# Routing's product and transposition as two pieces of VectorE's account; merges and output gating may wait a step

## The chip, the cores and the metric

The kernel runs on one core of one Trainium2 chip. The metric is the device time of one execution in microseconds (us), given as the median of several runs.

## The reference

Two batches of 1024 tokens of width 512 go through a layer norm, a causal attention with 32 heads of 16, and a feed-forward part whose output gates that of the attention. All is in float32.

```python
def attn(x):                                   # b, l, d = 2, 1024, 512; h, hd = 32, 16
    q, k, v = (heads(x @ W.T + b) for W, b in ((Wq, bq), (Wk, bk), (Wv, bv)))
    scores = einsum('bhqd,bhkd->bhqk', q, k) / sqrt(hd)
    att = softmax(where(causal, scores, -inf))
    return merge_heads(att @ v) @ Wo.T + bo

def ffn(x):                                    # E = 8 experts of rank R = 16, the best 2 used
    result = x @ W_base.T + b_base
    top_p, top_i = top_k(softmax(x @ W_gate.T), 2)
    route_w = sum(one_hot(top_i, 8) * (top_p / sum(top_p)))
    h = einsum('bnd,erd->bner', x, A)
    return result + einsum('bner,eor->bno', h * route_w[..., None], B) * 1.0

xn = layernorm(x)
return x + attn(xn) * silu(ffn(xn))
```

## The kernel before

Tokens are taken in chunks (b, c) of 512: two batches b, two chunks c of each. Attention is done in units (b, oc, c): eight heads (the output columns oc, 128 wide) for the queries of one chunk, over all keys up to them. A unit of c = 0 has 5 steps, one of c = 1 has 13. A step makes the scores of one or two tiles of 128 keys for four heads on TensorE (tiles `s`, line 1392), their exponentials on ScalarE (two instructions, `pt`, line 1401), and, where the tile lies on the diagonal, a multiplication with the causal mask on VectorE (two instructions). The product with the values (`av`, line 1442) follows one step later, so that TensorE has other work while ScalarE makes the exponentials. The last unit is cut otherwise. There are 144 steps in all, numbered from 0 in the variable `plan`.

The other work is spread over the steps as filling. It is written as generators, one for each piece of work: projections to q and k (products q1 to q7), to values, gate and output (p1 to p7), both by Strassen's scheme of seven products, with sums of operands (`asum`, `wqk`) made on VectorE ahead; the router's product (`ph`, copied to `hl` by ScalarE); layer norm. All filling products write to tiles of one PSUM pool (`ps_mm`) of two buffers, and VectorE, or ScalarE, reads them out.

The order of instructions is written out by a planner in Python when the program is built; the engines then run their instructions in that order. For each step n it emits the scores, the `av` matmuls of step n - 1 (with two copies from PSUM if these close a unit), the masks, and then calls `fill(n)`, which

- takes steps of generators that cost TensorE time (`Task` with a cost) until the step has its share, sorted by due time,
- then runs the list `later` of delayed pieces: (step, function),
- then takes steps of generators that cost TensorE nothing (layer norm, sums, routing) as long as VectorE's account allows. Such a generator is asked again at each `yield PAUSE`, and rests until the next step at `yield WAIT`,
- issues weight loads (`issue_parts`), at most six parts ahead.

VectorE's account is the class `Metered`, through which all VectorE instructions go: it adds 0.09 us and 1/930 us per element of a row for each. `late_by(n + 1, begins, more)` says by how much VectorE would be late for the masks of the next step if `more` us of work were added; `enough` is that question with 0.65. A piece in the list `patient` that is due in this very step is put off by one step when `enough()` is true.

The pieces that the change touches:

- `routed_task` picks the best two experts of every token by a chain of small VectorE operations (128x32), multiplies `hl` with the weights (`hw`, 128x512) and transposes the product in blocks (`hsq`). `hsq` is stored to DRAM and read back as `hwT` a step later (`place`), on the queue SP, which issues nearly all DMAs in order.
- `post` finishes a unit: `spread` brings the sums of the softmax to `dens`, `merge` takes reciprocals (`rc`) and joins the two halves of heads (`avs`, `oT`), `collect` brings the reciprocals back, `finish` multiplies. `merge` and `finish` are `patient`.
- `out_task` projects the attention's output in four blocks (i, j), in the order (0,0), (1,1), (0,1), (1,0). `final(i, j)` follows the read-out of the last product of a block: gating (`x<-x,g`), adding the residual (`x<-x,xr`), the store, and the load of the next residual tile `xr` (a pool of two buffers) if there is one left.
- `gate_task` has the same four blocks with a tanh on ScalarE (`sg`) and a multiplication; `apart`, behind the last q product of a unit, divides qT into two halves by two ScalarE activations (line 707).

Of the kernel before, what the change touches and what calls it, by code (L numbers as in the profile page):

```python
# [12 lines left out]
ALU = mybir.AluOpType  # L13
# [67 lines left out]
def direct(ctx, tc, sound, x, wq, wk, wv, wo, wb, wa, wg, wB, bq, bk, bv, bo, bb, out):  # L81
# [9 lines left out]
    nc = tc.nc  # L91
    ve = Metered(nc.vector)
# [117 lines left out]
    PAUSE = object()  # L210
# [552 lines left out]
    def out_task(k):  # L763

        _, b, c = stages[k]
        y, g = block_of(chunk_tile(b, c)), block_of(g_tiles[b, c])
        order = [(0, 0), (1, 1), (0, 1), (1, 0)]
        xts = {}

        def block(t, i, j):  # L770
            rows = slice(c * C + BK * i, c * C + BK * i + BK)
            return t[b, rows, BK * j : BK * j + BK].rearrange("(t p) o -> p t o", p=P)

        def load():
            i, j = order[len(xts)]
            xts[i, j] = sb.tile([P, 2, BK], F32, tag="xr", name=f"xr_{b}_{c}_{i}{j}")
            nc.sync.dma_start(out=xts[i, j], in_=block(x, i, j))

        def final(i, j):
            ve.scalar_tensor_tensor(y(i, j), y(i, j), 0.5, g(i, j), ALU.mult, ALU.mult)  # L780
            ve.tensor_tensor(y(i, j), y(i, j), xts[i, j], ALU.add)
            nc.sync.dma_start(out=block(out, i, j), in_=y(i, j))
            if len(xts) < 4:
                load()

        load()
        load()
        yield from block_task(k, y, final)
# [3 lines left out]
    def routed_task(b, c):  # L792


        hl = hls.pop((b, c))
        lg = hl[:, :, ER : ER + E]

        def each(name):
            return small.tile([P, TT], F32, tag=name, bufs=1, name=name)

        def every(name):
            return small.tile([P, TT, E], F32, tag=name, bufs=1, name=name)

        def over(t):
            return t.unsqueeze(2).to_broadcast([P, TT, E])

        mx = each("mx")
        ve.tensor_reduce(mx, lg, AX.X, ALU.max)
        pr = every("pr")
        ve.tensor_tensor(pr, lg, over(mx), ALU.subtract)  # L810
        yield WAIT
        nc.scalar.activation(pr, pr, AF.Exp)

        def top(p, n):
            m = each(f"m{n}")
            ve.tensor_reduce(m, p, AX.X, ALU.max)
            key = every(f"key{n}")
            ve.tensor_tensor(key, p, over(m), ALU.is_equal)
            ve.tensor_tensor(
                key, key, rev.unsqueeze(1).to_broadcast([P, TT, E]), ALU.mult  # L820
            )
            k = each(f"k{n}")
            ve.tensor_reduce(k, key, AX.X, ALU.max)
            ve.tensor_tensor(key, key, over(k), ALU.is_equal)
            ve.tensor_tensor(key, key, over(m), ALU.mult)
            return m, key

        m1, r1 = top(pr, 1)
        yield WAIT
        ve.tensor_tensor(pr, pr, r1, ALU.subtract)  # L830
        m2, r2 = top(pr, 2)
        ve.tensor_add(m1, m1, m2)
        ve.reciprocal(m1, m1)
        ve.tensor_add(r1, r1, r2)
        ve.tensor_tensor(r1, r1, over(m1), ALU.mult)
        yield WAIT
        hw = sb.tile([P, TT, ER], F32, tag="hw", bufs=1, name="hw")
        ve.tensor_tensor(
            hw.rearrange("p t (e r) -> p t e r", e=E),
            hl[:, :, 0:ER].rearrange("p t (e r) -> p t e r", e=E),  # L840
            r1.unsqueeze(3).to_broadcast([P, TT, E, R]),
            ALU.mult,
        )
        sq = sb.tile([P, NS, TT, SQ], F32, tag="sq", bufs=1, name="hsq")
        ve.transpose(
            out=sq.rearrange("p q t r -> p t q r"),
            in_=hw.rearrange("p t (q d) -> p t q d", q=NS),
        )
        hwT = sb.tile([P, NS, TT, SQ], F32, tag="hwT", bufs=2, name="hwT")
        scr = dram.tile([NS, SQ, NS, TT * SQ], F32, tag="hscr", name="hscr")  # L850
        nc.sync.dma_start(
            out=scr.rearrange("i d q m -> (i d) (q m)"), in_=sq.rearrange("p q t r -> p (q t r)")
        )

        def place():
            for q in range(NS):
                nc.sync.dma_start(
                    out=hwT[q * SQ : (q + 1) * SQ].rearrange("d i t r -> d i (t r)"),
                    in_=scr[:, :, q].rearrange("i d m -> d i m"),
                )  # L860

        later.append((now[0] + 1, place))
        hwTs[b, c] = hwT
        turned_at[b, c, "h"] = now[0]
# [410 lines left out]
    def late_by(n, begins, more):  # L1275


        free = ve.free + more
        if not 0 < n < len(plan):
            return free - begins  # L1280
        if plan[n - 1][3] and plan[n - 1][0] != units[-1]:
            free = max(free, begins + 2.0) + 1.3
        m = mask_time(n)
        if m:
            free = max(max(free, begins + 2.0) + m / 2, begins + 3.0) + m / 2
        return free - (begins + SV + 1.7 + 0.7)
# [11 lines left out]
    def fill(n):  # L1298


        nonlocal spent
        now[0], begun_at = n, spent
        within = 0 <= n < len(plan)
        causal_here = within and mask_time(n)
        for x in tasks:
            x.waiting = False
        for turn in [turn for turn in turns if turn[0] <= n]:
            turns.remove(turn)
            turn[1]()

        begin = len(plan) - 3
        even = (total - spent) / max(1, len(plan) - n)
        if n == len(plan) - 1:
            even = MM
        if n >= starts[units[-1]] - 8 and n < begin:
            even = sum(x.left for x in tasks if x.steps.__name__ not in ("whole_task", "rest_task"))
            even /= begin - n
        elif n < begin:
            even = min(even, (total - last_work - spent) / (begin - n))
        share = spent + even  # L1320
        if n >= 12:

            left = 0.0
            for x in tasks:
                if x.steps.__name__ in ("whole_task", "rest_task"):
                    continue
                left += x.left
                if x.due > n:
                    share = max(share, spent + left / (x.due - n))
        while True:  # L1330
            free = [x for x in tasks if x.cost and x.released(n)]
            if not free or free[0].due > n + 1:
                due = [x.steps.__name__ for x in tasks if x.cost and x.due <= n + 1]
                if due:
                    assert late, (n, due)
                    turn_late()
                    continue
                if not free or spent + (MM / 2 if causal_here or n < 12 else MM / 8) >= share:
                    break
            task = active[0] if active else free[0]  # L1340
            if (
                task.steps.__name__ == "qk_blocks_task" and task.due > n + 1
                and causal_here and spent - begun_at > 1.5 * MM
            ):

                break
            active[:] = [task]
            ve.ready = clock[0] + SV + spent - begun_at + MM
            cost = task.step()
            if cost is None or cost is WAIT:  # L1350
                task.waiting = True
                active.clear()
            else:
                spent += cost
        ve.ready = 0.0
        begins = clock[0] + max(2.3, SV + spent - begun_at)
        enough = lambda: late_by(n + 1, begins, 0.65) > 0
        for x in [x for x in later if x[0] <= n]:
            if x[0] == n and x[1] in patient and enough():
                continue  # L1360
            later.remove(x)
            x[1]()
        for x in [x for x in tasks if not x.cost]:
            if not x.released(n):
                continue
            said = PAUSE
            while said is not None and said is not WAIT:
                if enough() and x.due > n:
                    break
                said = x.step()  # L1370
            x.waiting = said is WAIT
        clock[0] = begins
        issue_parts()
        for _ in range(1 if active or len(plan) - 5 < n < len(plan) else 2):
            if late and (min(x[0] for x in late) <= n or not within):
                turn_late()
# [586 lines left out]
```

## Time and profile before

| | us |
|---|---|
| three runs, median (lowest, highest) | 601.71 (601.15, 601.98) |
| the profiled execution | 601.97 |
| its span, first to last instruction | 600.2 |
| busy: PE, VectorE (DVE), ScalarE (ACT) | 588.7, 391.6, 319.2 |
| mean granted TensorE clock | 0.996 |

The span is what the engines' records cover; 1.8 us of the profiled execution lie outside it. Matmuls (PE) overlap, and their ends are modelled: a busy PE is not proof of a PE at its peak, so steps are measured from start to start. In a row of the timeline stand the start, the duration, the engine, the line, the operation, the tiles (written <- read), the shape and the number of instructions run together; in brackets the idle time of the engine ahead of it and what ended it. All VectorE instructions have line 55, that of the account's helper, so they are told apart by their tiles. The costliest groups of VectorE are:

```profile
L55 DVE TENSOR_TENSOR pt<-pt,causal 128x512 f32<-128x512 f32 (+1 forms) x160 | 90.6, 582 | 64.9 <-ACT pt L1401 64.7
L55 DVE TENSOR_TENSOR g<-p,g 128x512 f32<-128x512 f32 x28 | 18.9, 686 | 16.8 <-PE p L220 16.5
L55 DVE SCALAR_TENSOR_TENSOR kT<-q,kT 128x256 f32<-128x256 f32 x39 | 16.5, 422 | 14.9 <-PE q L220 14.3
```

The first number behind the bar is the total busy time in us, the second the mean of one instruction in ns, the third the idle time ahead of them.

### The profile page before, as it was taken

What the parts mean: (1) busy time and instruction counts of PE and PEld (TensorE: products, weight loads), DVE (VectorE), ACT (ScalarE), POOL (GpSimd) and SP (SyncE); (2) the same over time, 40 slices, a digit from 0 to 9 for tenths busy, and PEclk for the clock granted to TensorE, in tenths of its full rate; (3) what the DMA queues carried; (4) which work ended last, traced back from release to release, by engine and by line L of the source; (5) the groups of instructions that cost most, each with busy time, mean ns of one, the idle gap of its engine ahead of it and who ended that gap; (6) DMA issues with size and microseconds to landing.
All of it is one profiled execution on the core that took longest, in us unless ns stands there. A gap on an engine that the chain in (4) does not pass through costs nothing.

```text
span 600.2 us, 18801 instructions
## 1 busy us (share of the span) xinstructions
PE 588.7 (98%) x8327; PEld 281.9 (47%) x8327; DVE 391.6 (65%) x821; ACT 319.2 (53%) x368; POOL 9.2 (2%) x26
## 2 busy tenths in 40 slices
PE   8999999999999999999999999999999999999994
PEld 7335344544445544444346544453444454455551
DVE  4546788287488857566487866664547865785742
ACT  2445454656666565556655545455565565565631
POOL 2000000000001000000000000000000000000000
PEclk9999999999999999999999999999999999999998
DMA  8523474247101534234133062430121013401101
GB/s 266 140 69 122 136 261 149 55 142 211 39 4 48 189 109 129 89 101 135 36 111 90 22 194 80 159 125 6 37 71 52 11 51 98 161 21 55 58 20 58
DMA packets 57929, 58.66 MB, mean 98 GB/s; under 512 B 8312, under 2 KB 49280, under 8 KB 57456
## 3 DMA queue, kind: packets, MB, share of 16 engines
q1 hardware_dynamic: 57824, 57.38, 31.0%
q8 instruction: 67, 1.10, 0.8%
q14 instruction: 22, 0.18, 0.1%
q10 hardware_dynamic: 16, 0.00, 0.0%
HBM read 43.24 MB, written 14.12 MB: 96 GB/s over the span
## 4 chain that ended last, share of the span: by engine, by line
PE 93%; DMA 3%; DVE 3%; issue 0%; SPq 0%; ACT 0%; DVEq 0%
PE s L1392 25%; PE av L1442 23%; PE p L220 20%; PE q L220 13%; PE ph L220 3%; PE po L220 2%; PE pv L220 2%; DMA kept<-wqk 1%; PE pq L220 1%; PE pk L220 1%; DMA dens<-den 1%; DMA x<-in_x_dram 1%; DVE wqk L55 1%; PE pq_first L330 1%; PE h L220 1%; PE pk_first L330 0%
## 5 line engine op out<-in xcount | busy, mean ns | idle before, releaser
L1401 ACT ACTIVATE pt<-s 128x1024 f32<-128x1024 f32 x288 | 279.2, 1021 | 230.2 <-PE s L1392 228.6
L1392 PE MATMUL s<-qT,kT 32*128 32x512 f32 (+3 forms) x1680 | 166.5, 490 | 0.1
L1442 PE MATMUL av<-pt,v 128*32 128x512 f32 (+3 forms) x1680 | 154.3, 467 | 0.9 <-DVE pt L55 0.6
L55 DVE TENSOR_TENSOR pt<-pt,causal 128x512 f32<-128x512 f32 (+1 forms) x160 | 90.6, 582 | 64.9 <-ACT pt L1401 64.7
L1392 PEld LDWEIGHTS s<-qT,kT 32*128 32x128 f32 x1680 | 72.4, 184 | 68.3 <-issue 47.3
L1442 PEld LDWEIGHTS av<-pt,v 128*32 128x32 f32 x1680 | 39.7, 108 | 93.6 <-issue 61.4
L220 PE MATMUL p<-wt,asum 128*32 128x256 f32 x960 | 58.2, 379 | 0.0
L220 PE MATMUL q<-asum,wqk 128*32 128x256 f32 x832 | 50.8, 379 | 0.0
L220 PEld LDWEIGHTS p<-wt,asum 128*32 128x32 f32 x960 | 31.0, 110 | 26.5 <-issue 9.9
L220 PE MATMUL q<-xnT,wqk 128*32 128x256 f32 x624 | 40.2, 379 | 0.0
L220 PEld LDWEIGHTS q<-asum,wqk 128*32 128x32 f32 x832 | 27.0, 110 | 25.1 <-issue 8.4
L55 DVE TENSOR_TENSOR g<-p,g 128x512 f32<-128x512 f32 x28 | 18.9, 686 | 16.8 <-PE p L220 16.5
L220 PEld LDWEIGHTS q<-xnT,wqk 128*32 128x32 f32 x624 | 20.9, 110 | 18.9 <-issue 5.1
L220 PE MATMUL p<-w,xnT 128*32 128x256 f32 x448 | 27.3, 379 | 0.0
L55 DVE SCALAR_TENSOR_TENSOR kT<-q,kT 128x256 f32<-128x256 f32 x39 | 16.5, 422 | 14.9 <-PE q L220 14.3
L55 DVE TENSOR_TENSOR x<-p,x 128x512 f32<-128x512 f32 x21 | 14.2, 688 | 15.0 <-PE p L220 15.0
L55 DVE TENSOR_TENSOR v<-p,v 128x512 f32<-128x512 f32 x21 | 14.1, 687 | 11.2 <-PE p L220 11.2
L220 PE MATMUL p<-w,asum 128*32 128x256 f32 x320 | 20.0, 379 | 0.0
L220 PEld LDWEIGHTS p<-w,xnT 128*32 128x32 f32 x448 | 14.5, 110 | 11.1 <-issue 3.3
L747 ACT ACTIVATE sg<-g 128x512 f32<-128x512 f32 x16 | 10.0, 630 | 16.9 <-DVE g L55 16.9
L707 ACT ACTIVATE qT<-qT,half 128x512 f32<-128x512 f32 x26 | 18.8, 722 | 0.4
L220 PE MATMUL ph<-wag_sb,xnT 128*32 128x136 f32 x512 | 17.2, 279 | 0.0
(132 smaller groups left out, 479.4 us busy)
## 6 DMA issues: line engine op xcount, KB each, us to landing
wt<-kept SPq DMA_DIRECT2D x40, 256.0 KB
x<-in_x_dram SPq DMA_DIRECT2D x16, 256.0 KB
scr<-sq SPq DMA_DIRECT2D x6, 512.0 KB
xnT<-scr SPq DMA_DIRECT2D x24, 128.0 KB
w<-in_wb_dram SPq DMA_DIRECT2D x12, 256.0 KB
xr<-in_x_dram SPq DMA_DIRECT2D x12, 256.0 KB
out_dram<-x SPq DMA_DIRECT2D x12, 256.0 KB
w<-in_wv_dram SPq DMA_DIRECT2D x9, 256.0 KB
```

The lines of the kernel that those rows point to most:

```text
L55: return getattr(self.engine, name)(*args, **named)
L220: nc.tensor.matmul(o[j : j + 32], lhsT=lhsT[:, j : j + 32] if len(lhsT.shape) == 2 else lhsT[:, j // 32], rhs=rhs, start=start, stop=stop,)
L330: nc.tensor.matmul(ps[:, cols], lhsT=w[:, k, :], rhs=xnT[:, k, cols], start=k == 0, stop=k == KC - 1)
L707: nc.scalar.activation(qT[:, par], qT[:, 0], AF.Copy, scale=half[:, par : par + 1])
L747: nc.scalar.activation(sg, g(i, j), AF.Tanh, scale=0.5)
L1392: nc.tensor.matmul(ss[s // 2][:, s % 2, col : col + w], lhsT=kT[rows, kt % TT * P : kt % TT * P + P], rhs=qTs[b, oc, c][rows, par, q0 : q0 ...
L1401: nc.scalar.activation(pt[:, 2 * pair : 2 * pair + 2], ss[pair], AF.Exp, scale=0.25)
L1442: nc.tensor.matmul(avs_now[par][32 * s : 32 * s + 32, q0 : q0 + w], lhsT=vs[b, kt][:, h * VS - HD * par : h * VS - HD * par + HP], rhs=pt[ ...
```

## The change

Three edits. In `out_task`, the gating of a block, its residual, store and load become a function `finish` that is put on `later` for this step and marked `patient`, so that it may be put off by one step; at the last block all that are still unfinished are run first. In `routed_task` a `yield PAUSE` stands between the product `hw` and the transposition `hsq`, so the account is asked again between them. In `fill`, the question to patient pieces is asked with 1.35 instead of 0.65 us.

```diff
@@ out_task
         def final(i, j):
-            ve.scalar_tensor_tensor(y(i, j), y(i, j), 0.5, g(i, j), ALU.mult, ALU.mult)
-            ve.tensor_tensor(y(i, j), y(i, j), xts[i, j], ALU.add)
-            nc.sync.dma_start(out=block(out, i, j), in_=y(i, j))
-            if len(xts) < 4:
-                load()
-
+            def finish():
+                ve.scalar_tensor_tensor(y(i, j), y(i, j), 0.5, g(i, j), ALU.mult, ALU.mult)
+                ve.tensor_tensor(y(i, j), y(i, j), xts[i, j], ALU.add)
+                nc.sync.dma_start(out=block(out, i, j), in_=y(i, j))
+                if len(xts) < 4:
+                    load()
+
+            if (i, j) == order[-1]:
+                for x in [x for x in later if x[1] in unfinished]:
+                    later.remove(x)
+                    x[1]()
+                finish()
+            else:
+
+                unfinished.append(finish)
+                patient.append(finish)
+                later.append((now[0], finish))
+
+        unfinished = []
         load()
         load()
         yield from block_task(k, y, final)
@@ routed_task
             r1.unsqueeze(3).to_broadcast([P, TT, E, R]),
             ALU.mult,
         )
+        yield PAUSE
         sq = sb.tile([P, NS, TT, SQ], F32, tag="sq", bufs=1, name="hsq")
@@ fill
-        enough = lambda: late_by(n + 1, begins, 0.65) > 0
+        enough = lambda more=0.65: late_by(n + 1, begins, more) > 0
         for x in [x for x in later if x[0] <= n]:
-            if x[0] == n and x[1] in patient and enough():
+            if x[0] == n and x[1] in patient and enough(1.35):
                 continue
             later.remove(x)
             x[1]()
```

## The prediction

> **What bounds the kernel now.** I read the page first, then the timeline of the matmul engine step by step, then the other engines around each step that is too long. A step is one run of score matmuls `s`, the `av` matmuls of the step ahead, and filling work; steps are counted from 0 at 14.94 us, the first `s` row of the chain.
>
> ```profile
> PE 588.7 (98%) x8327; PEld 281.9 (47%) x8327; DVE 391.6 (65%) x821; ACT 319.2 (53%) x368; POOL 9.2 (2%) x26
> PEclk9999999999999999999999999999999999999998
> PE 93%; DMA 3%; DVE 3%; issue 0%; SPq 0%; ACT 0%; DVEq 0%
> ```
>
> PE is busy 98% of the span at full clock and carries 93% of the chain that ended last. The change adds and removes no instruction on any engine, so only PE's waits can change. They are found by the length of steps: `s` takes 1.07, `av` 0.88, a filling unit (16 records of 256 columns) 0.86. Starts of `s` lie 3.79 apart with two units (504.80 to 508.59), 2.94 with one (508.59 to 511.53), 4.66 with three (352.84 to 357.50). Length is linear in the units, so moving units costs nothing by itself; what a step takes beyond is a wait. Those that the change can reach:
>
> ```profile
> 90.42 0.69 DVE L55 TENSOR_TENSOR hw<-hl,key 128x512 f32<-128x512 f32 x1
> 91.14 0.71 DVE L55 STREAM_TRANSPOSE hsq<-hw 128x512 f32<-128x512 f32 x1
> 91.78 0.72 DVE L55 TENSOR_TENSOR pt<-pt,causal 128x256 f32<-128x256 f32 x2
> 92.30 1.30 PE L1442 MATMUL av<-pt,v 128*32 128x512 f32 x8 [0.60 <-DVE pt L55]
> ...
> 310.37 0.69 DVE L55 SCALAR_TENSOR_TENSOR x<-x,g 128x512 f32<-128x512 f32 x1
> 311.09 0.69 DVE L55 TENSOR_TENSOR x<-x,xr 128x512 f32<-128x512 f32 x1
> 311.70 0.68 DVE L55 COPY oT<-av 128x512 f32<-128x512 f32 x1
> ...
> 312.90 0.75 DVE L55 TENSOR_TENSOR pt<-pt,causal 128x256 f32<-128x256 f32 x2
> 313.46 1.29 PE L1442 MATMUL av<-pt,v 128*32 128x512 f32 x8
> ```
>
> Step 15: `s` starts at 90.56, so `av` could start at 91.63, but VectorE did hw and hsq before the masks. The masks end at 92.50, and the step lasts 4.70: 0.90 lost. Step 73 is the same with the output gating (x<-x,g and x<-x,xr) in front: masks end at 313.65, `av` was due at 313.24, 0.45 lost. In both, the loss is the end of the second mask minus the time `av` was due, plus 0.04. That is my rule below.
>
> ```profile
> 508.59 1.15 PE L1392 MATMUL s<-qT,kT 32*128 32x384 f32 x16
> 509.83 1.94 ACT L1401 ACTIVATE pt<-s 128x1024 f32<-128x1024 f32 x2
> 511.53 1.42 PE L1392 MATMUL s<-qT,kT 32*128 32x512 f32 x8
> ...
> 360.32 2.07 PE L220 MATMUL q<-xnT,wqk 128*32 128x256 f32 x32
> 360.57 0.69 DVE L55 TENSOR_TENSOR v<-p,v 128x512 f32<-128x512 f32 x1 [1.73 <-PE p L220]
> ```
>
> A step with one unit is shorter than ScalarE's loop: the exponentials end at 511.77, the next `s` started at 511.53 and needs both, 0.28 lost. The last two rows show the other wait: filling products share two PSUM buffers, so a product waits until the one before the last is read out (read-out ends at 361.26, the buffer was wanted at 361.18, the step is 0.14 long).
>
> **The change, part by part.** I compared the order of instructions in the two programs as built. PE's order is the same through step 73.
>
> *Hw and hsq as two pieces.* In step 14 the masks now stand between them. They start 0.64 after hw's 90.42 at 91.06 (the gap between hsq and masks now), end at 91.78, against 91.63 plus the rule: 0.18 lost instead of 0.91. Gain 0.73. Hsq moves behind a read-out and four weight sums, to 93.6, and pushes the next masks to end at 95.55, due at 95.61: hidden. Its DMA to DRAM and the four that bring hwT back go one step later on SP, behind a store of sums; hwT is read from step 21 on (114 us), 15 us later. If the four sums took 0.1 more, the next `av` would lose that.
>
> *Output gating may wait.* In steps 71 to 73 it does, twice. The gating of the second block moves from step 71 to 72, that of the third from 72 to 73, where the fourth follows at once. The masks of step 72 come 0.8 earlier: the 0.45 is gone. The two sums of xnT finish in step 72 instead of 74, so the planner goes on with q6 in step 74 and the router products (ph) move from 74-76 to 93-95 and 102-103. That takes away 0.28 in step 75, where ph waited for ScalarE's copies. But q1's read-out now stands behind four gating operations. With 0.60 to 0.61 to the next independent operation, 0.72 where it needs the one before, 0.66 for a pair of masks: masks of 72 at 312.07, read-out of p3 312.73, gating 313.34 and 314.06, last sum 314.67, masks of 73 315.26 and 315.6, read-out of p4 315.92, gating 316.53, 317.25, 317.86, 318.58, q1's read-out 319.19 to 319.67. Queued behind it are the masks of 74. PE starts step 74 at 315.97; `s`, `av` and q2 end at 318.79, and q6 wants q1's buffer, free at 319.73: 0.94 lost. Low end 0.6 (all operations at 0.60), high 1.6: the fourth gating needs its tile xr, whose load on SP follows the second store and moves from 312.25 to 315.2; 256 KB behind a store landed in some 2.7, so at 317.9, wanted at 318.58. I take 0.94. On SP the last two stores hold back the load of dens by one us (at 318.94 now); its reader stands at 323.81: hidden.
>
> *What the new order of PE brings.* Step 123 and step 135 get a second unit. That saves 0.28 at 124; at 135 the chain of one-unit steps is one shorter (losses 0.27, 0.10, 0.17, 0.11, 0.14 in 136 to 140 become four), 0.13. Three things are lost. (a) Step 115 holds q5, q3 and q4 with large masks. As in step 21 the second mask starts 3.15 after the step, the next operation 3.76; q5 is read out twice (0.33 apart, 0.42 each), done at 4.51, while q4 wants its buffer at 1.96 + 2 x 0.86 = 3.68: 0.88. In step 101 without masks the same order costs 0.09 (read-out starts 0.15 after q5, ends 0.89 after it). (b) The division of qT into halves (two activations, 1.38 in the queue) moves to ScalarE in step 129, between one-unit steps: losses 0.28, 0.26, 0 in 129 to 131 become 0.28, 0.10, 0.27, so 0.11. (c) The second router chain falls under the gate of chunk (1,0), steps 105 to 109:
>
> ```profile
> 122.23 0.69 DVE L55 TENSOR_TENSOR g<-p,g 128x512 f32<-128x512 f32 x1
> ...
> 123.74 0.19 DVE L55 TENSOR_REDUCE m<-pr 128x4 f32<-128x32 f32 x1 [0.81 <-ACT pr L812]
> ...
> 128.83 0.18 DVE L55 TENSOR_TENSOR pr<-pr,key 128x32 f32<-128x32 f32 x1
> ...
> 130.87 0.69 DVE L55 TENSOR_TENSOR g<-p,g 128x512 f32<-128x512 f32 x1
> ```
>
> From these rows: read-out of p2 to the first reduction 1.51 (VectorE waits for two activations), first half of the chain 1.23, second half 2.04. With step 104 at 0: read-out of p2 in step 106 at 11.36, reduction 12.87, masks of 107 14.10 and 14.71, read-out of p6 15.32, multiplication 15.93, second half 16.53 to 18.57, the unit's two copies 18.57 and 19.17, masks of 108 19.78 to 20.53. The `av` of step 109 is due at 20.07: 0.50 lost, with 0 and 1.2 as ends (masks and chain each 0.3 to 0.6 off). Here the split of hw and hsq keeps 0.7 off the masks of 109.
>
> *Merges judged by 1.35* wait in steps 44 and 80, one step each. VectorE has 4.1 of work in step 45 and 0.7 less than before in 44; the copies queued behind start by 7.0 after step 45, their readers 8.7 after. On SP the store of the reciprocals is followed at once by the two loads that need it, and weight loads stand behind these, but weights are loaded six parts ahead (some 23 us). Cost 0; without that cover the 2.5 that SP once waited there now.
>
> Sum: gains 0.73 + 0.45 + 0.28 + 0.28 + 0.13 = 1.87; losses 0.94 + 0.88 + 0.09 + 0.11 + 0.50 = 2.52. Net +0.65 on the span of 600.2, which with 1.8 around it is the profiled 601.97. The median is 0.26 lower: 601.71 + 0.65 = 602.4.
>
> Each rate is taken between operations, and rows show the next one starting 0.08 before the 0.69 are over. The Trainium skill ("VectorE: DVE Perf Modes", "The DRAIN you can't avoid") has the next operation wait until the pipe is empty; by that the dozen operations ahead of q1's read-out would add some 0.7, and the sum would be +1.3. The rows decide.
>
> ```profile
> 90.00:98.00 8.00, 7.40 (x108) 4.07 (x104) 6.48 (x14) 3.51 (x4) 0.00 (x0) 1.00 0.53 161
> 312.00:320.00 8.00, 7.85 (x120) 4.29 (x112) 7.72 (x15) 3.88 (x4) 0.00 (x0) 1.00 0.63 195
> ```
>
> The windows around today's two longest waits show a granted clock (third number from the end) of 1.00. The skill's "TensorE: Matmul & The Clock Gate" ("A second HAM failure mode: psum-queue depth-cycling") warns that short idles from cycling PSUM buffers can drop the clock, which speaks against this change. Were each of the three new waits followed by 3.4 us at half clock, that page would add some 5, an estimate. Waits of this length did not do so here.
>
> **The rivals.** *A, slower: the router chain under the gate.* 19 small operations between masks of 1.3 each step; if the two activations come one exponential (1.94) later, the wait in step 109 is 2.4 instead of 0.50, and the time 604.3; with half of that 603.4. For it: VectorE has no slack from 106 to 112. Against: the built order has both activations ahead of the next exponentials. It decides from a wait of 1.05 on. *B, slower: the gating's tile xr lands late.* Each us past 318.58 delays q1's read-out by as much; from 0.55 late on the change is slower, at 1 late 603.4. For it: VectorE and SP wait for each other there; against: the landing time above. *C, faster: the new PSUM waits don't come,* because a buffer is given back earlier than I think: without 0.94 and 0.88 the time is 600.5, and without the 0.50 too, 600.0. Against: step 84 shows that wait.
>
> **How the numbers follow.** The forecast, 601.6 to 602.9, has 0.54; A 0.24, B 0.12, C 0.10. A difference of 0.2% (1.2 us) is about what a measurement can tell from none: faster than 600.5 is C, slower than 602.9 A and B. With the low ends of the two open terms (steps 74 and 109) the sum is -0.2, with the high ends +2.0. The range 600.6 to 604.2 goes past both, into A and B above, and leaves out most of C and the far end of A.
>
> **What would show it.** Step 15 should last about 4.0 instead of 4.70, step 73 3.80, step 74 about 4.7, step 109 4.3, step 115 5.5; steps 124 and 136 should lose nothing at `s`, 137 and 131 should. VectorE's read-out of q1 should start 3.2 after step 74. Wrong would be: a step that loses over 0.3 that is not named here, or steps 74 and 115 at 3.80 and 4.66.

## The result, and the profile after

The changed kernel is slower. Its median is 603.14 us (602.85 to 603.88, 12 runs), against 601.64 us for the kernel before, run beside it (12 runs). The ratio is 1.0029, with a 95% interval of 1.0021 to 1.0036. Its profiled execution took 603.88 and is the longest of the 12; its span is 602.1, against 600.2 before.

The page of the changed kernel, in the order of the prediction: busy time, granted clock, the chain that ended last, and the two groups of matmuls that write tile q.

```profile
PE 589.3 (98%) x8327; PEld 282.1 (47%) x8327; DVE 391.6 (65%) x821; ACT 319.0 (53%) x368; POOL 9.2 (2%) x26
PEclk9999999999999999999999999999999999999999
PE 90%; DVE 6%; ACT 1%; issue 1%; DMA 1%; SPq 0%; DVEq 0%
L220 PE MATMUL q<-asum,wqk 128*32 128x256 f32 x832 | 50.7, 379 | 0.7 <-DVE kT L55 0.7
L220 PE MATMUL q<-xnT,wqk 128*32 128x256 f32 x624 | 39.6, 379 | 0.9 <-DVE kT L55 0.8
```

The instructions are the same in number and kind, and the clock is full. What is new is VectorE's share of the chain, 6% instead of 3%, and idle time of PE ahead of q products, ended by kT, which is VectorE's read-out of an earlier q product.

To see all of it I took the loss of every step: its length, minus 2.075, minus 0.862 for each filling unit. This gives 0 for the undisturbed steps of 2.94, 3.80 and 4.66. The sum over all steps is 6.05 before and 7.70 after, 1.65 more. The rest of the 1.9 between the two spans lies outside the steps: the first `s` stands at 14.94 before and at 15.29 after, 0.35 later, and what follows the start of the last step is 0.08 shorter. The first `s` stands between 14.69 and 15.41 in the profiles of this study, so single profiles are compared by their steps and not by their spans.

| step | loss before | forecast | loss after |
|---|---|---|---|
| 15 (hw and hsq) | 0.90 | 0.18 | 0.28 |
| 73, 75 | 0.44, 0.26 | 0, 0 | 0, 0 |
| 74 (q6 waits for q1's buffer) | 0.02 | 0.94 | 0.95 |
| 101 (q4 waits for q5's buffer) | 0 | 0.09 | 0.32 |
| 109 (router chain) | 0 | 0.50 | 0.50 |
| 115 (q4 waits for q5's buffer) | 0.01 | 0.88 | 1.00 |
| 124 | 0.28 | 0 | 0 |
| 126 | 0 | 0 | 0.16 |
| 129 to 131 | 0.54 | 0.65 | 0.93 |
| 136 to 141 | 1.90 | 1.77 | 1.78 |
| all steps | 6.05 | 6.70 | 7.70 |

The timeline of the changed kernel at the places of these losses follows; its columns are those of the timelines before, and lines 1406, 1415 and 1456 are what lines 1392, 1401 and 1442 were. Step 15:

```profile
89.49 0.35 DVE L55 RECIPROCAL rc<-dens 128x32 f32<-128x32 f32 x1 [0.60 <-DMA dens<-den]
...
90.86 0.68 DVE L55 TENSOR_TENSOR hw<-hl,key 128x512 f32<-128x512 f32 x1
91.46 0.76 DVE L55 TENSOR_TENSOR pt<-pt,causal 128x256 f32<-128x256 f32 x2
92.02 1.30 PE L1456 MATMUL av<-pt,v 128*32 128x512 f32 x8
...
94.19 0.70 DVE L55 STREAM_TRANSPOSE hsq<-hw 128x512 f32<-128x512 f32 x1
```

The masks now follow hw at once, and hsq comes 2.7 later. From the start of hw to the end of the masks it is 1.36 (90.86 to 92.22), where it was 2.08 (90.42 to 92.50): 0.72 less. Ahead of hw VectorE waited 0.60 for the load of dens, where it was 0.51 before. That is why 0.28 is left.

Steps 73 and 74:

```profile
315.74 1.15 PE L1406 MATMUL s<-qT,kT 32*128 32x384 f32 x16
316.30 0.68 DVE L55 SCALAR_TENSOR_TENSOR x<-x,g 128x512 f32<-128x512 f32 x1
317.02 0.69 DVE L55 TENSOR_TENSOR x<-x,xr 128x512 f32<-128x512 f32 x1
317.63 0.68 DVE L55 SCALAR_TENSOR_TENSOR x<-x,g 128x512 f32<-128x512 f32 x1
318.35 0.69 DVE L55 TENSOR_TENSOR x<-x,xr 128x512 f32<-128x512 f32 x1
318.95 0.48 DVE L55 TENSOR_SCALAR kT<-q,b_sb 128x256 f32<-128x256 f32 x1
319.49 1.07 PE L220 MATMUL q<-asum,wqk 128*32 128x256 f32 x16 [0.74 <-DVE kT L55]
```

Four gating operations in a row stand between the start of step 74 and q1's read-out, which begins 3.21 after that start. The product q6 begins 0.06 after the read-out is over.

Steps 108 and 109:

```profile
450.72 0.18 DVE L55 TENSOR_TENSOR pr<-pr,key 128x32 f32<-128x32 f32 x1
...
452.76 0.69 DVE L55 COPY oT<-av 128x512 f32<-128x512 f32 x1
453.17 1.14 PE L1406 MATMUL s<-qT,kT 32*128 32x512 f32 x8
453.96 0.75 DVE L55 TENSOR_TENSOR pt<-pt,causal 128x256 f32<-128x256 f32 x2
454.52 1.29 PE L1456 MATMUL av<-pt,v 128*32 128x512 f32 x8 [0.21 <-DVE pt L55]
```

The second half of the router chain takes 2.04 (450.72 to 452.76), the two copies of the unit follow, and the masks end at 454.71. The `av` was due at 453.17 + 1.07 = 454.24.

Step 115:

```profile
478.71 0.69 DVE L55 TENSOR_TENSOR pt<-pt,causal 128x512 f32<-128x512 f32 x1 [0.16 <-ACT pt L1415]
479.63 0.69 DVE L55 TENSOR_TENSOR pt<-pt,causal 128x512 f32<-128x512 f32 x1 [0.23 <-ACT pt L1415]
480.24 0.42 DVE L55 SCALAR_TENSOR_TENSOR kT<-q,kT 128x256 f32<-128x256 f32 x1
480.57 0.41 DVE L55 SCALAR_TENSOR_TENSOR kT<-q,qT 128x256 f32<-128x256 f32 x1
481.13 1.07 PE L220 MATMUL q<-xnT,wqk 128*32 128x256 f32 x16 [0.79 <-DVE kT L55]
```

The step starts at 476.47. The masks wait for ScalarE's exponentials, and q5's two read-outs stand behind both masks. Q4 was wanted at 480.15 and starts at 481.13. The three losses that the forecast did not have, or not at this size, are in steps 101, 126 and 129:

```profile
423.32 1.91 PE L220 MATMUL q<-asum,wqk 128*32 128x256 f32 x32
424.44 0.42 DVE L55 SCALAR_TENSOR_TENSOR kT<-q,kT 128x256 f32<-128x256 f32 x1 [1.61 <-PE q L220]
...
425.34 1.07 PE L220 MATMUL q<-xnT,wqk 128*32 128x256 f32 x16
...
517.78 0.63 ACT L747 ACTIVATE sg<-g 128x512 f32<-128x512 f32 x1 [1.92 <-DVE g L55]
518.32 1.92 ACT L1415 ACTIVATE pt<-s 128x1024 f32<-128x1024 f32 x2
...
527.86 1.14 PE L1406 MATMUL s<-qT,kT 32*128 32x512 f32 x8
...
529.39 1.94 ACT L1415 ACTIVATE pt<-s 128x1024 f32<-128x1024 f32 x2 [2.14 <-PE s L1406]
```

In step 101 VectorE is free, and still q5 and q3 (the 32 records at 423.32) are followed by q4 2.02 later instead of 1.72: q5's first read-out starts 1.12 after q5, two read-outs take 0.75, and q4 starts 0.15 after them. In step 125 the product p4 is now the second unit of the step before, so the tanh of its block (`sg`) waits for a read-out and stands in ScalarE's queue ahead of the exponentials, which start at 518.32; the scores of step 126, which need the buffers that these read, take 1.30 from 520.11 on instead of 1.14. This is read from the rows; no run moved the tanh. In step 128 the exponentials start 1.53 after their scores.

### The profile page after: what moved, and what is told of

It reads as the page before. It is cut to its first block, busy times and chain, and to the rows that moved or that the text cites. A ratio compares the mean times of both kernels' runs of the same rounds, so it can differ in the third digit from the quotient of the medians.

```text
span 602.1 us, 18795 instructions
## 1 busy us (share of the span) xinstructions
PE 589.3 (98%) x8327; PEld 282.1 (47%) x8327; DVE 391.6 (65%) x821; ACT 319.0 (53%) x368; POOL 9.2 (2%) x26
## 4 chain that ended last, share of the span: by engine, by line
PE 90%; DVE 6%; ACT 1%; issue 1%; DMA 1%; SPq 0%; DVEq 0%
PE s L1406 24%; PE av L1456 22%; PE p L220 20%; PE q L220 12%; PE ph L220 2%; PE pv L220 2%; PE po L220 2%; DVE x L55 1%; PE pk L220 1%; PE pq L220 1%; DVE pt L55 1%; ACT pt L1415 1%; DMA x<-in_x_dram 1%; PE pq_first L330 1%; PE h L220 1%
## 5 line engine op out<-in xcount | busy, mean ns | idle before, releaser
L220 PEld LDWEIGHTS ph<-wag_sb,xnT 128*32 128x32 f32 x512 | 15.1, 110 | 4.7 <-issue 3.9
```

What stands on the lines that cost most here:

```text
L220: nc.tensor.matmul(o[j : j + 32], lhsT=lhsT[:, j : j + 32] if len(lhsT.shape) == 2 else lhsT[:, j // 32], rhs=rhs, start=start, stop=stop,)
```

## The experiments

All times of the table were taken beside runs of the kernel before (median 601.64 for the changed kernel; 601.71, on one chip, for pause_only, gating_thr, q1_first and masks115_last; on another chip 601.95 for q5_between, chain_later, three_fixes and pause_hold, and later 601.59 for pause_gating, pause_thr, pause_hold2 and pause_hold2_merge). "Loss" is the sum over all steps in one profile.

| kernel | median us | ratio to before (95%) | loss |
|---|---|---|---|
| changed kernel | 603.14 | 1.0029 (1.0021 to 1.0036) | 7.70 |
| pause_only | 600.94 | 0.9986 (0.9977 to 0.9995) | 5.12 |
| gating_thr | 604.07 | 1.0037 (1.0023 to 1.0051) | 8.15 |
| pause_gating | 601.06 | 0.9991 (0.9982 to 1.0000) | 5.13 |
| pause_thr | 600.76 | 0.9988 (0.9978 to 0.9997) | 5.28 |
| q1_first | 602.33 | 1.0009 (1.0000 to 1.0018) | 6.90 |
| masks115_last | 603.20 | 1.0024 (1.0013 to 1.0035) | 7.14 |
| q5_between | 603.08 | 1.0016 (1.0005 to 1.0027) | 6.68 |
| chain_later | 603.28 | 1.0021 (1.0010 to 1.0031) | 7.19 |
| three_fixes | 601.76 | 1.0000 (0.9989 to 1.0011) | 5.60 |
| pause_hold | 601.66 | 0.9999 (0.9987 to 1.0011) | 5.87 |
| pause_hold2 | 600.59 | 0.9980 (0.9971 to 0.9988) | 4.67 |
| pause_hold2_merge | 600.75 | 0.9987 (0.9978 to 0.9995) | 4.99 |

**Which edit brings what.** *pause_only* is the kernel before with the pause alone; *gating_thr* is the change without it.

```diff
@@ pause_only: routed_task (against before)
             ALU.mult,
         )
+        yield PAUSE
         sq = sb.tile([P, NS, TT, SQ], F32, tag="sq", bufs=1, name="hsq")
```

> Only the pause between the product and the transposition; PE's order is that of the kernel before in every step. My theory (the whole difference is PE's waits, step by step): step 15 shrinks from 4.70 to 4.0-4.1 us, the steps 73, 75, 84, 124, 129, 130 and 136 to 140 lose what they lose before, and the time falls by about 0.6 us (ratio 0.999). Rival (the later store and reload of hwT, or the other order on the DMA queue, costs something): a step from 16 to 25 is over 0.1 longer than before, and the time doesn't fall.

> The change without the pause: gating may wait, and merges are judged by 1.35. My theory: everything that made the change slower comes from here. Steps 74, 101, 109, 115, 126, 129 and 131 lose as in the changed kernel (0.95, 0.32, 0.5, 1.0, 0.16, 0.57, 0.25), step 15 again 0.9; the time is 0.6 to 0.7 us above the changed kernel, ratio to the kernel before 1.0035 to 1.004. At step 109 the transposition comes ahead of the masks again, 0.7 later masks, which I expect step 110 to hide. Rival (the pause is what hurts at step 109, by moving the transposition on): step 109 loses under 0.2.

The pause alone makes the kernel faster: step 15 loses nothing, all other steps lose what they lost before. In this profile VectorE also did not wait for dens, so not all of the 0.90 is the pause's. The two other edits together make it slower, with the losses of the changed kernel in 74, 101, 109 and 115 (0.94, 0.32, 0.50, 1.00), and 0.12 more in step 110, where without the pause hsq stands ahead of the masks. Step 15 lost 0.69 and not 0.9: hw started 3.45 after step 14, where it was 3.66 in the profile of before. The forecast had said that the pause keeps 0.7 off the masks there; only 0.12 of that would have been a loss.

*pause_gating* and *pause_thr* take these two edits one at a time, each with the pause.

```diff
@@ pause_gating (against the changed kernel)
-            if x[0] == n and x[1] in patient and enough(1.35):
+            if x[0] == n and x[1] in patient and enough():
@@ pause_thr (against the changed kernel): out_task.final as before
-            def finish():
...
+            ve.scalar_tensor_tensor(y(i, j), y(i, j), 0.5, g(i, j), ALU.mult, ALU.mult)
+            ve.tensor_tensor(y(i, j), y(i, j), xts[i, j], ALU.add)
```

> The changed kernel with the old question of 0.65 us: the pause between hw and hsq, and the output gating as a patient piece. As built it differs from before with the pause alone only in where one gating stands around step 88 and in the stores around it; PE's order is that of before. Theory (the loss comes from the new order of PE, which takes the gating and 1.35 together): no step from 73 to 131 loses what it loses in the changed kernel, the losses are those of the kernel with the pause alone (73 0.45, 75 0.26, 124 0.28, 109 and 115 nothing), ratio to before 0.9986 within what can be measured. Rival (making the gating patient is itself what costs): steps 74, 109 and 115 lose as in the changed kernel, ratio 1.002 or more.

> Before with the pause and with 1.35 us in the question to patient pieces (merges and finishes, no gating). As built it differs from before with the pause alone in one merge, which goes from step 44 to 45; PE's order is that of before. Theory as for the run above: losses as with the pause alone, ratio 0.9986 within what can be measured; the merge that waits costs nothing. Rival (the larger figure is itself what costs): 1.002 or more, with a loss in or behind step 45.

Neither costs anything: the losses of steps 73 to 131 are those of pause_only, each within 0.05. So the loss comes from the gating being patient and judged by 1.35 at once; only then does it wait in steps 71 to 73, and only then does PE get its new order. The merge that waits in step 44 costs nothing, as forecast.

**Step 74.** In *q1_first* the gating of the last block goes on the list that is run behind the step's products, so that it stands behind q1's read-out.

```diff
@@ q1_first: out_task.final (against the changed kernel)
             if (i, j) == order[-1]:
-                for x in [x for x in later if x[1] in unfinished]:
-                    later.remove(x)
-                    x[1]()
-                finish()
+                later.append((now[0], finish))
```

> The changed kernel, but the gating of the last block and those still open are put on the list of delayed pieces of the same step, so that q1 is read out ahead of the four gating operations of step 73. Theory (q6 waits in step 74 for the PSUM buffer that q1's late read-out holds): step 74 falls from 4.75 to 3.8-3.9, the masks of 74 still end at the same time, so step 75 loses 0.1 at most, and the time is some 0.8 below the changed kernel. Rival (step 74 waits for something else, such as the residual tile or the sums): step 74 stays at 4.5 or more.

```profile
316.44 0.47 DVE L55 TENSOR_SCALAR kT<-q,b_sb 128x256 f32<-128x256 f32 x1
316.83 0.68 DVE L55 SCALAR_TENSOR_TENSOR x<-x,g 128x512 f32<-128x512 f32 x1
...
318.71 1.04 PE L220 MATMUL q<-asum,wqk 128*32 128x256 f32 x16
```

That is the timeline of q1_first: the read-out is ahead of the gating, q6 starts without a wait, 2.82 after its step's start (315.89), and step 74 loses nothing. The cause is shown.

**Step 115.** Two ways of bringing q5's read-outs forward: *masks115_last* puts both masks behind the step's products, *q5_between* only the second.

```diff
@@ masks115_last (against the changed kernel)
-        masked(n, pts[n])
+        if n != 115:
+            masked(n, pts[n])
         fill(n)
+        if n == 115:
+            masked(n, pts[n])
@@ q5_between (against the changed kernel): masked() takes the pairs to do
-        masked(n, pts[n])
+        masked(n, pts[n], range(1) if n == 115 else range(2))
@@ q5_between: fill
             cost = task.step()
+            if n == 115 and second_mask:
+                second_mask.pop()
+                masked(n, pts[n], range(1, 2))
```

> The changed kernel, but VectorE does the masks of step 115 behind the read-outs of that step's filling. Theory (q4 waits for q5's buffer because q5's two read-outs stand behind the masks): step 115 falls from 5.66 to 4.7-5.0, as step 101 with the same three products and no masks, the av of step 116 loses under 0.2, and the time is some 0.7 below the changed kernel. Rival (three units in a step of large masks are too much for VectorE whatever the order): what step 115 gains is lost in step 116 or 117.

> The changed kernel, but in step 115 the second mask stands behind the two read-outs of q5 instead of ahead of them; nothing else moves, and PE's order is the same. Theory (q4 waits for the PSUM buffer of q5, because both masks stand ahead of q5's two read-outs): with one mask ahead of them the read-outs start 0.6 earlier than 0.61 behind the second mask, so that step 115 loses 0.05 to 0.2 instead of 1.00, the second mask ends well before the av of step 116 needs it (step 116 loses under 0.1), and the time falls by 0.8 to 0.9, to about 602.3. Rival (what moving both masks showed: with q5, q3 and q4 in one step VectorE has too much in it, and the loss only changes its step): step 115 and 116 together still lose 0.9 or more and the time stays at 603.1.

With both masks late the rival was right: step 115 fell from 1.00 to 0.32, but the masks now ran from 481.20 to 482.48, the `av` of step 116 was due at 481.74, and that step lost 0.78. With one mask in between the gain stays: 115 loses 0.32 and 116 only 0.01. The timeline of q5_between shows where the 0.32 comes from:

```profile
478.21 1.91 PE L220 MATMUL q<-asum,wqk 128*32 128x256 f32 x32
478.49 0.69 DVE L55 TENSOR_TENSOR pt<-pt,causal 128x512 f32<-128x512 f32 x1 [0.16 <-ACT pt L1420]
479.33 0.42 DVE L55 SCALAR_TENSOR_TENSOR kT<-q,kT 128x256 f32<-128x256 f32 x1
...
480.23 1.07 PE L220 MATMUL q<-xnT,wqk 128*32 128x256 f32 x16
```

It is step 101 again: the read-out starts 1.12 after q5, and q4 2.02 after it. With the masks out of the way the order q5, q3, q4 within one step costs 0.32 by itself; I had expected 0.05 to 0.2. In the medians the gain of 0.7 is not seen (603.08 beside 601.95 for the kernel before, 603.14 beside 601.64); the ratios, 1.0016 and 1.0029, differ by 0.8 us, but their intervals overlap. The reading rests on the steps.

**Step 109.** In *chain_later* the second half of the router chain rests one step.

```diff
@@ chain_later: routed_task (against the changed kernel)
         m1, r1 = top(pr, 1)
         yield WAIT
+        if now[0] == 107:
+            yield WAIT
         ve.tensor_tensor(pr, pr, r1, ALU.subtract)
```

> The changed kernel, but the second half of the second router chain rests one step more, so that it stands behind the masks of step 108, the read-out of the gate's last product and two multiplications instead of ahead of them. PE's order is the same. Theory (step 109 loses 0.50 because its av waits for masks behind the second half of the chain): step 109 loses 0 to 0.1, the time falls by 0.4 to 0.5 to about 602.65. Rival (the gate of chunk (1,0) fills VectorE from step 106 to 112 anyway, so the delay only goes one step on): steps 110 to 112 lose 0.3 or more in its place and the time stays within 0.2 of 603.1.

Step 109 loses 0.00: the cause is shown. But 0.32 of the 0.50 came back in steps 113 and 114, just after the steps (110 to 112) in which the rival expected it. In step 113 the planner now puts a merge where it had been in step 112, ahead of the two copies and the masks:

```profile
469.40 0.34 DVE L55 RECIPROCAL rc<-dens 128x32 f32<-128x32 f32 x1
...
470.76 0.68 DVE L55 COPY oT<-av 128x512 f32<-128x512 f32 x1
...
471.96 0.75 DVE L55 TENSOR_TENSOR pt<-pt,causal 128x256 f32<-128x256 f32 x2
472.55 0.84 PE L1458 MATMUL av<-pt,v 128*32 128x512 f32 x4
```

The masks end at 472.71, the `av` of step 114 was due at 472.47: 0.27 lost there, and 0.05 in step 113. The net gain is 0.18, too little for the time to show: with 603.28 it stays, as the rival said, where it was.

**All three.** *three_fixes* has q1_first, q5_between and chain_later together.

> The changed kernel with the gating of the last block put off (as in the run that brought step 74 to no loss), the second mask of step 115 behind the read-outs of q5, and the second half of the router chain behind the masks of step 108. If the three losses are independent, their sum goes: 0.95 + 0.85 + 0.45 = 2.25, time about 600.9, as fast as before with the pause alone (600.94), and not faster, because the new order of PE keeps its other losses (steps 101, 126 and 129, together 0.77) against what it saves (73, 75, 124 and the chain to 140, together 1.1). If they are not independent (VectorE is short of time as a whole from step 104 on), 601.5 or more.

In the steps the three gains add up: steps 74, 109 and 115 lose 0.00, 0.00 and 0.32, with the 0.32 of steps 113 and 114. The time, 601.76, lies over the 601.5 from which I would have called them not independent. It is that of the kernel before (1.0000), and 0.86 above what I expected. Of this 0.17 is what step 115 kept beyond 0.15, 0.32 is the merge, and 0.31 goes with the kernel before, which has 601.95 beside these runs instead of 601.64. Even with its three worst waits mended, the new order is no gain over before. By the steps it is behind the pause alone (5.60 lost against 5.12); the intervals of the two ratios overlap.

**Gaining what the gating was good for.** Step 73 loses 0.45 before. *pause_hold* keeps the order of PE and holds just the gating of the second block for one step. *pause_hold2* also puts the last block's gating behind q1's read-out.

```diff
@@ pause_hold: out_task.final (against pause_only)
+            if now[0] == 71:
+                held.append((i, j))
+                return
+            for i, j in held + [(i, j)]:
...
@@ pause_hold2: out_task.final (against pause_hold)
+            if now[0] == 73:
+                later.append((73, lambda: gating(i, j)))
+                return
...
```

> The kernel before with the pause between hw and hsq, and with the output gating of one block (the second, in step 71) held until the next block's gating in step 72; PE's order is that of before. Theory (step 73 loses 0.45 only because this gating stands ahead of the masks of step 72): step 73 loses nothing, 74 and 75 stay as they are (0.02, 0.26), time 600.94 - 0.45 = 600.5. Rival (as in the changed kernel, what is put off comes back as a wait of a product for its PSUM buffer in step 74, or the fourth xr tile, now loaded 2.6 later, lands late): step 74 loses 0.4 or more and the time stays at 600.9.

> The kernel before with the pause, the output gating of the second block held from step 71 to step 72 as in the run that lost 0.59 in step 74, and the gating of the last block put behind the read-out of q1 in step 73. PE's order is that of before. Theory (a put-off gating costs only what is queued behind it: masks in step 73, q1's read-out in 74): both lose nothing, 0.45 less than with the pause alone, ratio to before 0.9986 - 0.0007 = 0.998. Rival (VectorE is full from step 71 to 75, so the masks of step 74 or the read-out of q2 come late in their turn): step 75 or 76 loses 0.4 or more beyond 0.26.

In step 74 the first run went as its rival said, the second as its theory said. The time of the first is some 0.8 over that of the pause alone by the ratios; in its profile 0.63 of this stands in steps 15 and 16, which are taken up below. The timeline of pause_hold, then that of pause_hold2:

```profile
318.27 0.48 DVE L55 TENSOR_SCALAR kT<-q,b_sb 128x256 f32<-128x256 f32 x1
...
318.81 0.90 PE L220 MATMUL ph<-wag_sb,xnT 128*32 128x136 f32 x24 [0.36 <-DVE kT L55]
```

```profile
316.73 0.47 DVE L55 TENSOR_SCALAR kT<-q,b_sb 128x256 f32<-128x256 f32 x1
...
318.28 0.88 PE L220 MATMUL ph<-wag_sb,xnT 128*32 128x136 f32 x24
```

Both steps start within 0.02 of each other (315.43 and 315.45). With the gating ahead of q1's read-out the next product waits for the buffer, and step 74 loses 0.59. With the read-out first it waits for nothing: 73 loses 0, 74 loses 0.02, 75 keeps its 0.26. It has the lowest median of the study, and with its ratio of 0.9980 it beats both the kernel before and the changed one. That it is faster than the pause alone is read from the steps; the intervals of the two ratios overlap.

**The rest of step 15.** From profile to profile, step 15's loss followed the time at which the load of dens landed. In pause_hold it was 0.56, after this wait:

```profile
89.19 0.35 DVE L55 RECIPROCAL rc<-dens 128x32 f32<-128x32 f32 x1 [0.90 <-DMA dens<-den]
```

In pause_only the same instruction started at 88.25 without a wait, and nothing was lost. *pause_hold2_merge* puts this merge behind the masks of step 14.

```diff
@@ pause_hold2_merge: post (against pause_hold2)
+        hold = n + 3 + wait == 13
-        later.append((n + 3 + wait, merge))
-        later.append((n + 4 + wait, collect))
+        later.append((n + 3 + wait + hold, merge))
+        later.append((n + 4 + wait + hold, collect))
```

> The run above, and the first merge (the reciprocals of the first unit and what follows them) goes from step 13 to 14, behind the masks, with the collection of the reciprocals one step later too. The loss in step 15 has gone from 0 to 0.56 between runs of the same order, with the time at which the load of dens landed ahead of that merge. Theory (the masks of step 14 are late by what VectorE waits for dens): step 15 loses nothing in any run, and the time is 0 to 0.4 below the run above, with less spread. Rival (a merge in step 14 makes the masks of step 15 late, or the reciprocals land too late): step 16 loses 0.3 or more.

Step 15 loses 0.01, but this is one profile, and pause_hold2 lost nothing there either, so the first half of the theory is not tested by it. A loss of 0.33 turned up in step 18; the rival had named reciprocals that land too late, but had put the loss in step 16:

```profile
100.46 0.01 DVE L55 LOAD_MASK_SELECT rb<-avs  x1 [1.85 <-DMA avs<-back]
...
104.10 1.07 PE L220 MATMUL q<-xnT,wqk 128*32 128x256 f32 x16
```

The reciprocals were collected one step later, VectorE waited 1.85 for them, and q5's read-outs, which stand behind that wait and four other operations, came at 103.21 and held q4 back.

## Why the prediction was right or wrong

The time lies inside the range (600.6 to 604.2). The likeliest case, no measurable difference, did not come; the case that I gave 0.36, slower, did. The median is 0.74 above 602.4. None of the rivals was the reason: the forecast's own steps came, and its sum was too small by 1.0 in the profiles (1.65 of loss in place of 0.65), or by 0.85 between the medians (1.50). That the range holds the time is in part luck: it went up to 604.2 for rivals A and B, which did not come. Its signs of being wrong did not come either: every step or group of steps with 0.3 or more of new loss is one that it names.

- *Hw and hsq.* Right in place and in size: 0.72 from the start of hw to the end of the masks for 0.73. The profiles differ by only 0.62 because hw started later. I had taken the wait for dens (0.51 in the profile of before) as fixed; it varies, and the loss with it. Where dens landed early nothing was lost with the pause; in pause_only hw started 3.04 after step 14 instead of 3.66, so without the pause some 0.28 would be lost there, an estimate from these rows (0.90 - 0.62). Hsq's later place cost 0.06 at most (step 16).
- *Output gating.* Right. The 0.45 of step 73 and the 0.26 of 75 went, step 74 lost 0.95 for 0.94, q1's read-out started 3.21 after the step for 3.2. Tile xr was in time: `x<-x,xr` at 318.35 did not wait. Rival B is out.
- *Step 109.* 0.50 for 0.50, and chain_later showed the cause. The first reduction stood 1.50 after the read-out ahead of it (445.59 to 447.09), where I had 1.51. Rival A, to which I gave 0.24, is out.
- *Step 115.* 1.00 for 0.88. Q5's read-outs ended 4.51 after the step's start, as worked out, and q4 was due at 3.68. The 0.88 thus had only 0.05 for the hand-over, the time from the end of the read-outs to q4's start, which took 0.15. Rival C is out: these waits came in full.
- *Step 101 failed in size:* "in step 101 without masks the same order costs 0.09 (read-out starts 0.15 after q5, ends 0.89 after it)". It cost 0.32. The read-out started 0.26 after q5 (1.12 after its start, 0.86 of work), the second ended 1.01 after q5, and q4 needed 0.15 more. The end was 0.12 later than in my row (0.89), and my 0.09 had only 0.06 for the hand-over (0.89 is 0.03 beyond q3's 0.86).
- *Step 126 was missing.* I had followed the units that move up behind the new one of step 123 on PE alone. On ScalarE this puts the tanh ahead of the exponentials: 0.16, as the rows have it.
- *Steps 129 to 131.* "Losses 0.28, 0.26, 0 become 0.28, 0.10, 0.27" was right for the last two (0.11, 0.25). Step 129 lost 0.57, because the exponentials of step 128 started 1.53 after the scores, where the same place in masks115_last had 1.24. Why is open.
- *Merges.* Right: nothing was lost in steps 44 to 54, and behind 80 only the 0.15 that step 84 lost before, now in step 83.
- *The sum,* then: 0.23 (101), 0.16 (126), 0.29 (129), 0.12 (115), 0.11 (15) and 0.06 (16) make 0.97 of the 1.0. Most of this stands on the side of the losses. The gains were removals of waits that I could see; the losses were waits that I built up from rows. The hand-over of a PSUM buffer, which I took as 0.05 or 0.06 throughout, was right in step 74 and 0.09 to 0.10 too small in 101 and 115; step 126 left out an engine, and what makes step 129 late stays open.

The two rules that the prediction weighed did not decide anything. The Trainium skill ("VectorE: DVE Perf Modes", "The DRAIN you can't avoid") would have each operation start when the pipe is empty; at 317.02 and 317.63 an operation of 0.69 was followed by an independent one after 0.61, and q1's read-out came where the rows had put it. The same section adds that an operation which is not held starts earlier, which I had left out, and sends the reader on to "Two Vector instructions with no wait between them"; with that the rows agree. "TensorE: Matmul & The Clock Gate" ("A second HAM failure mode: psum-queue depth-cycling") warns of a clock drop behind such waits; the windows around the two longest show a granted clock (third number from the end) of 1.00:

```profile
315.00:325.00 10.00, 9.26 (x148) 4.89 (x144) 8.33 (x17) 3.94 (x5) 0.00 (x0) 1.00 0.54 161
475.00:485.00 10.00, 9.21 (x156) 4.86 (x148) 6.42 (x14) 4.48 (x5) 0.00 (x0) 1.00 0.01 2
```

## What to carry to other kernels

When a piece of work is allowed to wait, look at what will be queued behind it in its new place: here a put-off gating removed 0.45 as a late mask and came back as 0.95 as a late read-out, and the same deferral with the read-out put first cost nothing. A planner that counts each engine's time, but not how long two PSUM buffers are held, can trade a visible wait on one engine for an unseen one on another. And when the new order of a busy engine is costed, each moved unit has to be followed onto the engines that serve it (the tanh of step 126), and the hand-overs (0.06 to 0.15 from read-out to matmul) have to be counted, because they are all on the side of the losses.

## What the runs showed of the hardware

- The load of dens was issued at about the same time in pause_only and in pause_hold (83.81 and 83.68) but let the reciprocal start by 88.25 in the first and at 89.19 in the second. So the loss of step 15 was anything from 0 to 0.56 in profiles of kernels that have the pause.
- From the end of the read-out that frees a PSUM buffer to the start of the waiting product it took 0.06 in step 74 and 0.15 in steps 101 and 115. What makes the difference was not tried.
- The late start of the exponentials in step 128 came back in six of the seven profiled kernels with the new order of PE (0.57 or 0.58 lost in step 129), but not in masks115_last (0.28). The records show no instruction ahead of it on ScalarE and no late operand. In the six late profiles a packet of the queue q14 ("instruction" in the profile) starts 0.6 to 0.9 after the late start; in masks115_last the packet near it starts 1.56 before the step. Whether the two belong together was not tried. It was not settled.
